# Narrow filler products in every softmax unit, and one tile's transposes and logits moved into the first dense layer

## The chip, the cores and the metric

The kernel runs on one core of a Trainium2 chip. The metric is the device time in microseconds of one execution; the time of a version is the median of its runs. Smaller is better. The engines are called PE (TensorE, matrix products), DVE (VectorE), ACT (ScalarE), POOL (GpSimd) and SP (SyncE, which here only issues DMAs).

## The reference

The input x has 8 sequences of 512 tokens with 1024 features, 4096 tokens in all, in f32. Four layers follow each other, each added to its input after a layer norm without weights:

```python
x = x + attn_a(layernorm(x), qkvw, qkvb, ow, ob)   # softmax attention, 32 heads of 32
x = x + ffn(layernorm(x), weight, bias, centroids, assignments)
x = x + attn_b(layernorm(x), bv_q, bv_k, bv_v)     # sigmoid attention, causal, 4 heads of 256
x = x + ffn(layernorm(x), weight, bias, centroids, assignments)
```

The two parts that the change touches are these:

```python
# attn_a
qkv = x @ attn_qkvw + attn_qkvb
scores = einsum('bhqd,bhkd->bhqk', q, k) / sqrt(32)
ctx = einsum('bhqk,bhkd->bhqd', softmax(scores), v)
out = ctx @ attn_ow + attn_ob
# ffn
dots = softmax(x @ centroids.T / 0.1)              # 64 clusters
hits = dots > 0.01
query_sel, cluster_sel = any(hits, axis=1), any(hits, axis=0)
row_sel = cluster_sel[assignments]
out = where(query_sel[:, None] & row_sel[None, :], x @ weight.T + bias, 0)
```

Which outputs of the first ffn layer are kept depends on the hits of all 4096 tokens. So no row of that layer can be finished before the last tile of 128 tokens has its logits, though its dense product can be begun.

## The kernel before, in words

**Stages.** The program is one body, `block_body`. It runs softmax attention with its output projection (to about 2673 us of the profiled execution), the first dense layer (about 2673 to 3000), the sigmoid attention, and the second dense layer. A tile is 128 tokens, there are 32 of them (0 to 31), four to a sequence.

**Products.** All big products (the q, k, v projections, the output projection, the dense layers) are in f32 and, after the first sequence, use a scheme with seven products for a two by two block product; `gather` adds their results up on DVE. In the code a "product" is one call of `nc.tensor.matmul` with 128 contracted rows. In the trace an f32 product is two passes, each a weight load and a matmul.

**The softmax loop** (L1003 on) goes over 64 units, one for four heads of one sequence. Unit n has four steps i. In step i, `rows_step` for unit n+1 (L873) makes the scores of 128 queries with all keys, and DVE takes their maxima (L874). `keys_step` for unit n (L901, L904) makes the scores of 128 keys with all queries, adds the maxima as a shift, and ACT takes exp of them (L906). Both use four matmuls side by side, on 32 rows of the array each, and share one PSUM buffer of four banks, `sc`, so each must wait until the other's scores are consumed. `values_step` (L928) and `normalize` (L940) make the context and the denominators; their matmuls are also four side by side, on 32 columns each. Once per unit, `turn_max` (L886 to L893) transposes the maxima, kept as three bf16 parts, through PE and copies them to SBUF.

**Filler.** Between those steps PE gets other work from a queue, `Filler`. Each piece has a weight, roughly its microseconds. The queue holds the projections of unit n+2 (`project_pieces`), the products of the output projection of the previous sequence (`out_products`), and for one finished tile at a time its norm, its transposes (L277) and its cluster logits, first by cluster (`logitsT`, L325), then by token (`logits`, L333). `filler.plan` splits a unit's queue over nine fillings by fixed shares, and the calls of `between` take them: in step 0 one before the turn of the maxima, one after it and one at the end of the step; in each other step one before `keys_step` and one after. The order of instructions on every engine is the program's order; nothing reorders it.

**Full and narrow form.** `product` (L548 to L556) writes a product either as one matmul on all 128 columns (L556) or, if the flag `narrow[0]` is set, as four matmuls on 32 columns each, side by side (L554). The flag is set by `between(False, form=...)` only for the fillings at the end of steps 0 and 2, which stand just after `values_step`, from unit 1 on. The transposes of `turn_max` and of tiles and the logits by token never go through `product`.

**The last output stage.** After the loop, four rounds (L1073 to L1089) do the output projection of the last two pairs of tiles (28 with 29, 30 with 31), with the pieces of the tiles that became ready. Round 0 has the tiles 26 and 27. Round 3 has 28 and 30. `filler.mix(pieces, first, step)` puts pieces into the queue at the given places. The tiles 29 and 31 are yielded at the end and laid among dense products by `to_rows` (L1403), whose list says which steps run and how many dense products follow them. A tile's transposes are copied by ACT into `nT`, which has one buffer; it leaves by a DMA from POOL's queue (L846), and only then can the next tile's copy start. The buffers of `ps_m` in PSUM, three of one bank, serve the products, the transposes and the logits alike. After the last logits, `rows_pieces` counts the hits, selects the rows, and the gates of the dense layer can begin.

Of the kernel before, what the change touches and what calls it, by code (L numbers as in the profile page):

```python
# [13 lines left out]
F32 = mybir.dt.float32  # L14
BF16 = mybir.dt.bfloat16
# [7 lines left out]
P = 128  # L23
# [3 lines left out]
TPB = S // P  # L27
NTILE = NT // P

HEADS_A, HD_A = 32, 32  # L30
# [6 lines left out]
NCL = 64  # L37
# [267 lines left out]
class Clusters:  # L305
# [5 lines left out]
        self.hits = fixed.tile([P, NCL], F32, name=f"hits_{name}")  # L311
        self.logits = {}

    def pieces(self, t, xT, later=None, width=NCL):

        nc, (b, i), st, ps_m = self.stage.nc, divmod(t, TPB), {}, self.stage.ps_m

        def by_cluster():  # L320
            acc = ps_m.tile([P, P], F32, tag="mm", name="logitsT")
            for c in range(NC):
                for j in range(NCL // width):
                    rows = ts(c % 2 * (NCL // width) + j, width)
                    nc.tensor.matmul(  # L325
                        acc[rows, :], self.cT[:, c, ts(j, width)], xT()[:, c, :], start=(c < 2), stop=(c >= NC - 2)
                    )
            st["lT"] = self.pool.tile([P, P], F32, tag="lT", name=f"lT_{self.name}_{t}")
            nc.scalar.copy(st["lT"], acc)

        def by_token():
            acc = ps_m.tile([P, NCL], F32, tag="mm", name="logits")
            nc.tensor.matmul(acc, st["lT"], self.stage.cst.twice, start=True, stop=True)  # L333
            if i == 0:
                self.logits[b] = self.pool.tile([P, TPB, NCL], F32, tag="lg", name=f"lg_{self.name}_{b}")
            nc.scalar.activation(self.logits[b][:, i, :], acc, AF.Copy, scale=INV_TEMP)
            if i == TPB - 1:
                steps = self.softmax(b)
                if later is None:
                    for step in steps:  # L340
                        step()
                else:
                    later(steps)

        return [(1.3, by_cluster), (0.25, by_token)]
# [61 lines left out]
def softmax_attention(tc, cst, stage, filler, clusters, pools, dr, late, args):  # L407
# [11 lines left out]
    nc, small, ps_m = tc.nc, stage.small, stage.ps_m  # L419
# [128 lines left out]
    narrow = [False]  # L548
# [281 lines left out]
    def tile_pieces(t, r, blocks=False):  # L830


        st = {}

        def xn():
            if "n" not in st:
                st["n"] = npool.tile([P, H], F32, tag="n1", name=f"n1_{t}")
            return st["n"]

        def xT():  # L840
            if "T" not in st:
                st["T"] = npool.tile([P, NC, P], F32, tag="nT", name=f"nT_{t}")
            return st["T"]

        def keep():
            nc.gpsimd.dma_start(dr.xT1[t], st["T"].rearrange("p c t -> p (c t)"))  # L846

        def box():
            if "box" not in st:
                st["box"] = npool.tile([P, NC, P], F32, tag="nT", name=f"nB_{t}")  # L850
            return st["box"]

        def fetch():
            nc.sync.dma_start(xT().rearrange("p c t -> p (c t)"), dr.xT1[t])

        if blocks:
            turn = stage.block_pieces(xn, box, dr.xT1[t]) + [(0.0, fetch)]
        else:
            turn = stage.turn_pieces(xn, xT, keep, vector=False)
        return (  # L860
            stage.norm_pieces(lambda: r, xn, scalar=True) + turn,
            clusters.pieces(t, xT, None if t >= NTILE - TPB else held.extend, width=HD_A),
        )

    def rows_step(n, qt):
# [10 lines left out]
    def split_max(n):  # L876

        st = state[n]
        part, rest = parts[n % 2], small.tile([P, TPB, GH], F32, tag="rest", name="rest")
        nc.vector.tensor_copy(part[:, :, :, 0], st["nmax"])  # L880
        nc.vector.tensor_tensor(rest, st["nmax"], part[:, :, :, 0], ALU.subtract)
        nc.vector.tensor_copy(part[:, :, :, 1], rest)
        nc.vector.tensor_tensor(rest, rest, part[:, :, :, 1], ALU.subtract)
        nc.vector.tensor_copy(part[:, :, :, 2], rest)

    def turn_max(n):  # L886

        st = state[n]
        tp = ps_m.tile([P, TPB, P], BF16, tag="mm", name="tpm")
        for qt in range(TPB):  # L890
            nc.tensor.transpose(tp[:, qt, :], parts[n % 2][:, qt, :, :].rearrange("p h c -> p (h c)"), cst.ident_h)
        st["shift"] = shiftp.tile([P, S], BF16, tag="shift", name=f"shift_{n}")
        nc.scalar.copy(st["shift"], tp.rearrange("p t q -> p (t q)"))  # L893

# [55 lines left out]

    places = [0]

    def between(sides=True, form=False):


        if sides:
            for _ in range(-(-len(side) // places[0])):
                side.popleft()()
            places[0] -= 1
        narrow[0] = form  # L960
        filler.take()
        narrow[0] = False

    def mix_tile(near, wait):
        norm, logits = tiles.popleft()(blocks=wait)
# [30 lines left out]
    pieces = project_pieces(1)  # L996
# [3 lines left out]
    run(enumerate(side))  # L1000
    side.clear()
    split_max(0)
    for n in range(units):  # L1003
        b, g = divmod(n, NC)
        ahead = n + 2
        if n == NC - 2:
            weights.fill(W_BUFS)
        if n == NC:
            ows.fill(OW_BUFS)
        count = 0  # L1010
        if n > NC:
            count = OUT_SHARES[(n - 1) % half] if n <= units - NC else LAST_SHARES[n - units]
        products = [next(outs) for _ in range(count)]
        if ahead < units:
            if g == NC - 2:
                side.extendleft(reversed(left_tasks(b + 1)))
            filler.add(weave(project_pieces(ahead), products), mark=ahead)
        else:
            filler.add(weave([], products))
        ready.extend(waiting)  # L1020
        waiting.clear()
        if tiles:
            mix_tile(n == units - 1, ahead < units)
        for c in OUT_SUMS.get(n, ()):
            side.extend(ow_sum_tasks(c))
        if b + 1 < B:
            if g == 0:
                norms = deque(norm_tasks(b + 1))
            if g < 2:
                run(enumerate(norms.popleft()))  # L1030
            if norms:
                side.extend(norms.popleft())
        side.extend(held)
        held.clear()
        filler.plan(FILLER_SHARES)
        places[0] = TPB + 1
        for i in range(TPB):
            if n + 1 < units:
                rows_step(n + 1, i)
            if i == 0 and n > 0:  # L1040
                sum_step(n - 1, TPB - 1)
            between()
            if i == 0:
                turn_max(n)
                between()
            if i == TPB - 1:
                sum_step(n, i - 1)
            keys_step(n, i)
            if i == 1:
                sum_step(n, i)  # L1050
            if i == 0 and n > 0:
                values_step(n - 1, 1)
                if ready:
                    by_cluster, by_token = ready.popleft()
                    run([by_cluster])
                    filler.mix([by_token], 6, 1)
                normalize(n - 1)
            if i == 2:
                values_step(n, 0)
            between(False, form=i in (0, 2) and n > 0)  # L1060
        if n + 1 < units:
            split_max(n + 1)
        if ahead < units:
            filler.until(ahead)
    sum_step(units - 1, TPB - 1)
    values_step(units - 1, 1)
    normalize(units - 1)
# [5 lines left out]
    for i, (start, end) in enumerate(((0, 4), (4, 8), (8, 10), (10, 14))):  # L1073
        ready = [make() for make in tiles]
        tiles.clear()
        for idx, k in order[start:end]:
            filler.add(last_pairs[k][0][idx])
            if idx == 0:
                filler.mix([last_pairs[k][2]], 2 + 4 * k, 1)
        for k, (norm, logits) in enumerate(ready):  # L1080
            filler.mix(norm[:2], 6 * k, 3)
            filler.mix(norm[2:], 11 + 8 * k, 2)
            filler.mix(logits, 15 + 8 * k, 3)
        filler.mix(late[i], 2, 4)
        filler.drain()
        run(enumerate(held))
        held.clear()
        if i < 3:
            yield  # L1089
    yield [make() for make in tiles]  # L1090


def ste_sign(nc, pool, w, n, name, hard):
# [234 lines left out]
def block_body(tc, long, dr, args, out):  # L1328
    x, xT_in, qkvw, qkvb, ow, ob, bv_q, bv_k, bv_v, wT, fbias, cT, assign = args
    nc = tc.nc  # L1330
# [66 lines left out]
    dense_stack = ExitStack()  # L1397
    dense1 = Dense(stage, weights, dense_pools(dense_stack), None, dr.xT1, dr.x1, hits1, sel)
    dense1.load_turned(0)
    (norm0, logits0), (norm1, logits1) = next(attention)  # L1400
    dense1.sums(0)
    dense1.load_turned(1)

    def to_rows(steps, hits, dense):
# [4 lines left out]
        for step, n in steps + [(count, 4), (rows, 3)]:  # L1409
# [4 lines left out]
    rest = [(0.0, step) for step in weight_sums[4:]]  # L1414
    left_over = to_rows(
        [
            (norm0[:2] + rest[:2], 8), (norm0[2:] + norm1[:1] + rest[2:], 4), (norm1[1:2] + logits0[:1], 3),
            (logits0[1:], 3), (norm1[2:], 3), (logits1[:1], 2), (logits1[1:], 8),
        ], hits1, dense1,
    )  # L1420
    a_outer.close()
# [228 lines left out]
```

## Time and profile before

| | us |
|---|---|
| median of 3 runs | 3823.99 (3821.19 to 3825.94) |
| the profiled execution, its own time | 3821.42 |
| its span, first to last instruction | 3819.7 |
| PE busy | 3760.0 (98%) |
| DVE busy | 2538.5 (66%) |
| ACT busy | 916.4 (24%) |
| POOL busy | 598.0 (16%) |

By stretch of the span, with what PE was busy in each:

| stretch, us | what runs | PE busy, us |
|---|---|---|
| 69 to 2598 | the softmax loop | 2506.96 of 2529 |
| 2598 to 2673 | the last output stage | 62.92 of 75 |
| 2673 to 3000 | the first dense layer | 325.73 of 327 |

The mean granted clock of PE was 0.998. PE executed 23,942 matmuls and as many weight loads. The start of a matmul in the trace is recorded and its end is modelled, so consecutive matmuls overlap in it; how fast they follow each other is read from their starts. In a timeline row, `128*32` means 128 active rows and 32 active columns of the array, and the size after it is that of the moving operand. A bracket at the end of a row gives idle time before it and what ended that.

### The profile page before, as it was taken

What the parts mean: (1) busy time and instruction counts of PE and PEld (TensorE: products, weight loads), DVE (VectorE), ACT (ScalarE), POOL (GpSimd) and SP (SyncE); (2) the same over time, 40 slices, a digit from 0 to 9 for tenths busy, and PEclk for the clock granted to TensorE, in tenths of its full rate; (3) what the DMA queues carried; (4) which work ended last, traced back from release to release, by engine and by line L of the source; (5) the groups of instructions that cost most, each with busy time, mean ns of one, the idle gap of its engine ahead of it and who ended that gap; (6) DMA issues with size and microseconds to landing.
All of it is one profiled execution on the core that took longest, in us unless ns stands there. A gap on an engine that the chain in (4) does not pass through costs nothing.

```text
span 3819.7 us, 58523 instructions
## 1 busy us (share of the span) xinstructions
PE 3760.0 (98%) x23942; PEld 2087.6 (55%) x23942; DVE 2538.5 (66%) x3495; ACT 916.4 (24%) x996; POOL 598.0 (16%) x585
## 2 busy tenths in 40 slices
PE   8999999999999999999999999998999999999999
PEld 4445555555555555555555555543444467774444
DVE  4767676767667667766866766665788844456556
ACT  1222222222222222222222222222111144430000
POOL 1222111111111111111111111111000045530000
PEclk9999999999999999999999999999999999999999
DMA  5335455645655455465455554356566665553332
GB/s 168 118 120 171 127 145 146 186 138 145 187 144 145 151 173 147 130 188 149 132 172 152 145 146 125 114 156 230 160 176 176 170 186 193 190 187 133 132 132 99
DMA packets 674490, 590.59 MB, mean 155 GB/s; under 512 B 268072, under 2 KB 519984, under 8 KB 674224
## 3 DMA queue, kind: packets, MB, share of 16 engines
q1 hardware_dynamic: 645120, 482.77, 44.4%
q0 software_dynamic: 24784, 88.36, 6.0%
q10 hardware_dynamic: 4320, 15.73, 1.0%
q8 instruction: 190, 3.11, 0.4%
q14 instruction: 76, 0.62, 0.1%
HBM read 452.48 MB, written 134.25 MB: 154 GB/s over the span
## 4 chain that ended last, share of the span: by engine, by line
PE 91%; DVE 6%; DMA 1%; issue 1%; ACT 0%; POOL 0%; SPq 0%; DVEq 0%; ACTq 0%; POOLq 0%
PE mm L556 34%; PE dense L1236 19%; PE sc L901 7%; PE sc L873 7%; PE mm L554 7%; PE av L928 6%; PE csc L1295 4%; PE o L1314 4%; PE logitsT L325 1%; PE sc L904 1%; DVE nmax L874 1%; PE den L940 1%; PE tp L277 1%; DVE sum L917 1%; DVE ln_st L227 1%
## 5 line engine op out<-in xcount | busy, mean ns | idle before, releaser
L874 DVE TENSOR_REDUCE nmax<-sc 128x4 f32<-128x2048 f32 x256 | 586.0, 2289 | 299.7 <-PE sc L873 299.7
L906 ACT ACTIVATE pT<-sc 128x2048 f32<-128x2048 f32 x256 | 480.8, 1878 | 1160.5 <-PE sc L904 1155.5
L915 POOL TENSOR_TENSOR sum<-pT,pT 128x1024 f32<-128x1024 f32 x128 | 304.9, 2405 | 765.2 <-ACT pT L906 723.4
L556 PE MATMUL mm<-xT,w 128*128 128x256 f32 x1716 | 416.4, 388 | 1.6 <-DVE rden L943 1.6
L556 PEld LDWEIGHTS mm<-xT,w 128*128 128x128 f32 x1716 | 312.8, 190 | 125.4 <-issue 35.3
L901 PE MATMUL sc<-qk,qk 32*128 32x512 f32 x2048 | 292.6, 641 | 15.1 <-DVE nmax L874 14.6
L917 DVE TENSOR_TENSOR sum<-sum,pT 128x2048 f32<-128x2048 f32 x128 | 292.0, 2282 | 0.8 <-ACT pT L906 0.8
L873 PE MATMUL sc<-qk,qk 32*128 32x512 f32 x2048 | 291.9, 640 | 0.2
L142 DVE TENSOR_TENSOR u<-dense,u 128x512 f32<-128x512 f32 x223 | 149.2, 686 | 185.4 <-PE dense L1236 168.4
L928 PE MATMUL av<-pT,v 128*32 128x512 f32 x2048 | 246.2, 598 | 0.0
L1236 PE MATMUL dense<-sum,s 128*128 128x512 f32 x512 | 232.1, 594 | 2.6 <-DVE s L1183 2.6
L556 PEld LDWEIGHTS mm<-w,xT 128*128 128x128 f32 x1640 | 192.6, 192 | 51.1 <-issue 41.2
L556 PE MATMUL mm<-s,w 128*128 128x256 f32 x852 | 204.6, 386 | 0.0
L556 PE MATMUL mm<-w,xT 128*128 128x128 f32 x1640 | 204.6, 278 | 0.0
L556 PEld LDWEIGHTS mm<-s,w 128*128 128x128 f32 x852 | 156.9, 190 | 68.2 <-issue 29.3
L144 DVE SCALAR_TENSOR_TENSOR qk<-mm,qkvb_s,qk 128x256 f32<-128x256 f32 x224 | 107.6, 480 | 124.9 <-PE mm L556 83.9
L556 PE MATMUL mm<-ow,ctxT 128*128 128x512 f32 x354 | 176.6, 616 | 0.3 <-DMA ow<-o_T 0.2
L1236 PE MATMUL dense<-wT_s,dT_b 128*128 128x512 f32 x384 | 171.4, 593 | 1.7 <-DMA dT_b<-xT 1.7
L1236 PE MATMUL dense<-wT_s,dT_a 128*128 128x512 f32 x384 | 171.0, 593 | 0.0
L556 PEld LDWEIGHTS mm<-w,s 128*128 128x128 f32 x1344 | 156.7, 192 | 19.4 <-issue 19.4
L556 PE MATMUL mm<-w,s 128*128 128x128 f32 x1344 | 166.8, 277 | 0.0
L1236 PEld LDWEIGHTS dense<-sum,s 128*128 128x128 f32 x512 | 96.4, 190 | 123.4 <-issue 112.3
(244 smaller groups left out, 4932.5 us busy)
## 6 DMA issues: line engine op xcount, KB each, us to landing
w<-in_qkvw SPq DMA_DIRECT2D x252, 256.0 KB, 3.0
ow<-o_T SPq DMA_DIRECT2D x240, 256.0 KB, 3.7
w<-qk_T SPq DMA_DIRECT2D x224, 256.0 KB, 2.7
ow<-in_ow SPq DMA_DIRECT2D x180, 256.0 KB, 3.2
w<-v_T SPq DMA_DIRECT2D x112, 256.0 KB, 2.7
x<-in_x SPq DMA_DIRECT2D x32, 512.0 KB, 4.9
dT_a<-xT SPq DMA_DIRECT2D x32, 512.0 KB, 5.9
x_a<-x SPq DMA_DIRECT2D x32, 512.0 KB, 6.8
```

Of the source, the lines that this page charges most:

```text
L554: nc.tensor.matmul(out[ts(j, HD_A)], lhsT[:, ts(j, HD_A)], rhs, **flags)
L556: nc.tensor.matmul(out, lhsT, rhs, **flags)
L873: nc.tensor.matmul(sc[:, h, :], st["q"][rows, ts(qt, P)], st["k"][rows, :], start=True, stop=True)
L874: nc.vector.tensor_reduce(st["nmax"][:, qt, :], sc, AX.X, ALU.max, negate=True)
L901: nc.tensor.matmul(sc[:, h, :], st["k"][rows, ts(kt, P)], st["q"][rows, :], start=True, stop=False)
L906: nc.scalar.activation(pT, sc, AF.Exp, scale=SCALE_A)
L915: nc.gpsimd.tensor_tensor(st["sum"][:, h, :], st["pT", 0][:, h, :], st["pT", 1][:, h, :], ALU.add)
L917: nc.vector.tensor_tensor(st["sum"], st["sum"], st["pT", kt], ALU.add)
L928: nc.tensor.matmul(st["av"][rows, :], st["v"][:, kt, rows], pT[:, h, :], start=(kt == 0), stop=(kt == TPB - 1))
L1236: nc.tensor.matmul(st["acc"], st["left"][LEFT[k]][:, c, :], self.w[RIGHT[k]][:, c, :], start=(c == 0), stop=(c == half - 1),)
L1295: nc.tensor.matmul(sc[:, AT_OFF[i] : AT_OFF[i] + n], k[:, c, ts(i, P)], xT[:, c, i * P :], start=(c == 0), stop=(c == 1),)
L1314: nc.tensor.matmul(acc[:, j - jj, :], at[:, start : start + P], self.v[b * TPB + i][:, cols], start=(i == 0), stop=(i == j),)
```

## The change

The flag `narrow[0]` is set before the loop and cleared after it, so all filler products of all units are in the narrow form; `between` loses its argument. `turn_max` uses `product` with the identity as the moving operand in place of PE's transpose, and its PSUM tile is f32 instead of bf16. The tiles of the softmax stage pass `product` on to `pieces`, which uses it for the logits by token. In the last output stage, the places where a tile's transposes and logits are put change, and tile 30's transposes and logits are held back from round 3 and yielded, to stand first in the list of `to_rows`. The counts of dense products in that list change with it: 35 places pass before the hits are counted, instead of 31.

```diff
-    def pieces(self, t, xT, later=None, width=NCL):
+    def pieces(self, t, xT, later=None, width=NCL, product=None):
...
-            nc.tensor.matmul(acc, st["lT"], self.stage.cst.twice, start=True, stop=True)
+            (product or nc.tensor.matmul)(acc, st["lT"], self.stage.cst.twice, start=True, stop=True)
...
-            clusters.pieces(t, xT, None if t >= NTILE - TPB else held.extend, width=HD_A),
+            clusters.pieces(t, xT, None if t >= NTILE - TPB else held.extend, HD_A, product),
...
-        tp = ps_m.tile([P, TPB, P], BF16, tag="mm", name="tpm")
+        tp = ps_m.tile([P, TPB, P], F32, tag="mm", name="tpm")
         for qt in range(TPB):
-            nc.tensor.transpose(tp[:, qt, :], parts[n % 2][:, qt, :, :].rearrange("p h c -> p (h c)"), cst.ident_h)
+            part = parts[n % 2][:, qt, :, :].rearrange("p h c -> p (h c)")
+            product(tp[:, qt, :], part, cst.ident_h, start=True, stop=True)
...
-    def between(sides=True, form=False):
+    def between(sides=True):
...
-        narrow[0] = form
         filler.take()
-        narrow[0] = False
...
     split_max(0)
+    narrow[0] = True
     for n in range(units):
...
-            between(False, form=i in (0, 2) and n > 0)
+            between(False)
...
             filler.until(ahead)
+    narrow[0] = False
     sum_step(units - 1, TPB - 1)
...
             filler.mix(norm[:2], 6 * k, 3)
-            filler.mix(norm[2:], 11 + 8 * k, 2)
-            filler.mix(logits, 15 + 8 * k, 3)
+            if (i, k) == (3, 1):
+                left_over = norm[2:], logits
+            else:
+                filler.mix(norm[2:], (13 if i < 3 else 9) + 8 * k, 2)
+                filler.mix(logits, (18 if i < 3 else 14) + 8 * k, 4)
...
-    yield [make() for make in tiles]
+    yield [left_over] + [make() for make in tiles]
...
-    (norm0, logits0), (norm1, logits1) = next(attention)
+    (turn, logits), (norm0, logits0), (norm1, logits1) = next(attention)
...
-            (norm0[:2] + rest[:2], 8), (norm0[2:] + norm1[:1] + rest[2:], 4), (norm1[1:2] + logits0[:1], 3),
-            (logits0[1:], 3), (norm1[2:], 3), (logits1[:1], 2), (logits1[1:], 8),
+            (norm0[:1] + turn + norm0[1:2], 5), (logits[:1] + rest[:2], 3), (logits[1:], 2), (norm0[2:] + norm1[:1] + rest[2:], 4), (norm1[1:2] + logits0[:1], 3),
+            (logits0[1:], 3), (norm1[2:], 4), (logits1[:1], 3), (logits1[1:], 8),
```

## The prediction

> **What bounds the kernel now.** I read the page's busy shares and chain first, then the waits of TensorE, then its timeline in one softmax unit and at the turn to the first dense layer.
>
> ```profile
> PE 3760.0 (98%) x23942; PEld 2087.6 (55%) x23942; DVE 2538.5 (66%) x3495; ACT 916.4 (24%) x996; POOL 598.0 (16%) x585
> PE 91%; DVE 6%; DMA 1%; issue 1%; ACT 0%; POOL 0%; SPq 0%; DVEq 0%; ACTq 0%; POOLq 0%
> q8 instruction: 190, 3.11, 0.4%
> PE sc L901 <- DVE nmax L874: 14.6, 12, 3.0
> ```
>
> PE is busy 98% and is 91% of the chain. Its longest wait is 14.6 us in 12 places. So the end is set by how closely PE's instructions follow each other, which the timeline shows (start, length, line, tiles, active rows*columns, size of the moving operand, count; a row's length overlaps the next, so I take differences of starts):
>
> ```profile
> 1517.33 1.92 PE L928 MATMUL av<-pT,v 128*32 128x512 f32 x16
> 1519.07 1.05 PE L554 MATMUL mm<-s,w 128*32 128x256 f32 x16
> 1519.93 1.06 PE L554 MATMUL mm<-w,xT 128*32 128x128 f32 x32
> 1520.92 1.14 PE L873 MATMUL sc<-qk,qk 32*128 32x512 f32 x8
> 1521.99 1.16 PE L556 MATMUL mm<-w,xT 128*128 128x128 f32 x8
> 1522.98 1.95 PE L556 MATMUL mm<-w,s 128*128 128x128 f32 x16
> 1524.77 1.06 PE L556 MATMUL mm<-w,xT 128*128 128x128 f32 x8
> 1525.76 1.14 PE L901 MATMUL sc<-qk,qk 32*128 32x512 f32 x8
> ...
> 1530.99 1.99 PE L556 MATMUL mm<-xT,w 128*128 128x256 f32 x8
> 1532.82 0.39 PE L891 MATMUL tpm<-ident_h,parts 128*128 128x128 bf16 x4
> 1533.04 1.95 PE L556 MATMUL mm<-xT,w 128*128 128x256 f32 x8
> 1534.92 1.14 PE L901 MATMUL sc<-qk,qk 32*128 32x512 f32 x8
> ```
>
> Three forms alternate: scores on 32 rows (R), full products (F), and products in four 32-column parts (C). An f32 product is two passes; a C pass is four instructions. The trace's starts, over all rows of the phase, give:
> - One pass of N=256 takes 216 ns and of N=512 429 ns in F and C alike. At N=128, F takes 112 (mean 111.7) and C 109.
> - R to either form costs 109 ns. Then F pays 104 ns on its first pass (1521.99 to 1522.98 is 0.99, 8x0.112 is 0.90); C pays 24 (1517.33 to 1519.07 is 1.74, 4x0.429 is 1.716).
> - Back to R: F pays 93 ns (1524.77 to 1525.76), C 113 (1519.93 to 1520.92 is 0.99, 8x0.109 is 0.872).
> - The turn of the maxima is 4x56 ns, and the F pass after it is 56 late: 1533.04 to 1534.92 is 1.88, 8x0.216 plus 0.093 plus 0.056.
>
> Then the turn to the dense layer:
>
> ```profile
> 2663.15 0.60 PE L277 MATMUL tp<-ident,n 128*128 128x128 f32 x4
> 2667.04 0.43 PE L333 MATMUL logits<-twice,lT_a 128*128 128x64 f32 x2 [3.29 <-ACT nT L279]
> 2667.53 1.93 PE L325 MATMUL logitsT<-nT,cT_s 128*32 128x128 f32 x32
> 2672.99 3.60 PE L1236 MATMUL dense<-wT_s,dT_a 128*128 128x512 f32 x8
> ```
>
> Tile 30's copies into nT wait for tile 28's nT to leave by DMA, and PE idles 3.29 us. The 32 matmuls after it take 1.93 us against 1.08 elsewhere: the windows show a clock of 0.74 there.
>
> [...] each change costs about 0.1 us, whichever two forms meet. [...] the first passes show 104 and 24. [...] the four of a C pass start 7 ns apart. [...] The full bf16 turn ran at 56 ns; no run here shows bf16 on 32 columns.
>
> **The change, part by part.** (a) *Narrow in all units.* Of a unit's nine fillings seven are F now, in six visits between R steps (the first two share one with the turn). Over 64 units the built order gives 378 R-to-F and 383 F-to-R changes, of which 3 each stay. The number of changes is the same afterwards[...]. Loads: 375x(104-24) = 30.0 us less. Way back: 380x(113-93) = 7.6 us more. Net -22.4.
>
> (b) *Pitch.* 3328 full N=128 passes become narrow: 3328x(111.7-109.2) = -8.3. The 2568 passes of N=256 and 700 of N=512 change by nothing; they are most of PE's time, and the C rows of before show the pitch is kept over 16 passes.
>
> (c) *Turn of the maxima.* Four bf16 transposes become four products of four parts, into f32. PE streams the same columns, and eight instructions 7 ns apart just fit in 56 ns: I take 4x56 and no delay after it[...], -64x56 = -3.6. Upper bound: the f32 pitch, 4x109, which is 64x(436-280) = +10.0 instead. The ScalarE copy stays 128x512 (0.59 us).
>
> (d) *Logits by token.* 25 of them stand in the loop: two passes of 56 ns, after which F waits 56 twice for its load. Narrow hides it: -2.8. Four tiles' transposes in the last units now stand between C rows: +0.2.
>
> Sum of PE in the loop: -22.4-8.3-3.6-2.8+0.2 = -36.9. Some is not kept: in about 26 places PE waits already (25 us in all), behind DVE or a copy that PE's gain does not hasten. A unit gains 0.58 us in 39; such a run of DVE work is some 10 us, so 26x0.15, about 4 us, goes into longer waits. Kept: -33. Of the L901 starts nine in ten stand 0.34 us or more after the reduce that frees their banks, more than one stretch gains.
>
> (e) *Last output stage.* Before, waits of 4.0 us lie at tiles 26 and 27 (1.84, 0.58, 0.99, 0.60). Moved two products later, their first transpose waits 0.4; the next still waits for DVE's L762 at 2606.2, and tile 27's copies for tile 26's DMA. I take -1.5. At the last part, tile 28's transposes go ahead by two products, but product 9 then needs the bank that DVE frees at 2657.26, wherever PE stands: eight products are done then, not ten. From there eight products (6.9), logits (1.4) and tile 30's transposes (0.9) reach the dense layer at 2666.5 instead of 2672.99: -6.5. Tile 30's logits, now inside it, return 1.5; the wait of 0.63 for tile 29 goes. Moved with tile 30 are two copies and one 512 KB DMA on POOL's queue; tile 29's root stands ahead of that DMA, so nothing on POOL is delayed. Sum -7.1.
>
> (f) *What is late next.* At the last logits 27 dense products are done, not 23. DVE's order does not move with them: softmax and hits, then the sums of pair 1, 6.6 us after the last logits (2697.97 to hits 2702.66, plus an addition and two sums). PE needs that sum after five products, 4.5 us: a new wait of 2.1. Then rows, gates and pair 2's sums: from the selection's copies to that sum 22.2 us before, 21.6 now; PE has 26 products from the count, not 30, and waits 1.9. Together +4.0, so this turn gives -3.1.
>
> Total -36. The profiled execution, 3821.4 us with a span of 3819.7, becomes 3785.4; the median of the three runs is 2.6 above it, so I forecast 3788.
>
> **The rivals.** *The turn is dear:* [...] 13.6 us less gain, 3802. [...] *The gain is taken up by waits:* DVE, 66% busy, sets the units, and the gain in the loop falls to about a third, 3809. Against: only 25 us of waits in 2,530, and L901's slack. *Slower, by instruction fetch:* the loop's PE instructions double, by the built order from 39,000 to 80,000, and q8 brings them in packets of 16 KB, 256 instructions of 64 bytes. A narrow N=128 pass takes 8 in 109 ns and empties a packet's worth in 3.5 us; 3728x8/256 = 116 such packets fall in N=128 work, where now one stretch is under 4 us. A packet took 0.9 to 1.8 us, 1.08 in the median. Were that exposed at each, +125: 3913. It decides from 36/116 = 0.31 us a packet. Against: narrow rows of 32 run at 109 with no gap, also where a fetch falls beside them. *It does not do what it says:* the built order shows the F rows of the loop turned into C, so this is out, save for a clock that falls under narrow work; ACT's and DVE's lengths and the clock (1.00) are the same in narrow stretches.
>
> **How the numbers follow.** Forecast, with its turn between 56 and 80 ns, 3788: 0.66. Dear turn, 3802: 0.14. Taken up, 3809: 0.12. Slower, 3913: 0.05. A clock or other loss that just cancels the gain, 3824: 0.03. Low end: the loop's gain kept whole (-36.9), no new waits in dense (-7.1), all 4.0 us at tiles 26 and 27 gone instead of 1.5, and the runs' own spread of 2.8: 3775. High end: the dear turn with 5 us of further waits, 3807. About 0.2% (7.6 us) is what a measurement can tell from no change: faster 0.92, same 0.03, slower 0.05.
>
> **What would show it.** Right: F rows of the loop gone to L554; first passes after R 24 ns late; N=128 at 109; turn and its successor 56 apart; nearly as many mode changes; the loop's last denominators about 33 us earlier; the 3.29 us gone, and two waits of dense for DVE's s of about 2 us. Wrong: gaps in PE that no semaphore ends, at block distances; a pitch of turn near 109; the wait of L901 for nmax grown by tens of us; a clock below 1.00 in the loop.

## The result, and the profile after

The changed kernel takes 3833.97 us (median of 17 runs, 3826.48 to 3839.74), the kernel before 3823.62 beside it (17 runs). The ratio is 1.0028, 95% interval 1.0022 to 1.0035: slower by about 10 us (0.3%), and 46 us above my forecast of 3788. The profiled execution took 3832.04, with a span of 3830.3 and a clock of 0.995 (before 3821.42, 3819.7, 0.998).

The lines of the page after, which answer to those of before:

```profile
PE 3742.1 (98%) x44666; PEld 1865.3 (49%) x44666; DVE 2539.7 (66%) x3495; ACT 916.3 (24%) x996; POOL 603.0 (16%) x585
q8 instruction: 352, 5.77, 0.6%
PE 88%; DVE 8%; issue 2%; DMA 1%; SPq 0%; ACT 0%; POOL 0%; DVEq 0%; ACTq 0%; POOLq 0%
```

PE is busy 17.9 us less, as it should be, and yet the end is later. In the chain "issue" is 2% where it was 1%: time in which PE waited for nothing that the profile shows. The instruction queue q8 brought 352 packets instead of 190. The waits of TensorE say where (us in total, times, longest):

```profile
PE mm L554 <- issue: 19.9, 14, 3.8
PE sc L902 <- DVE nmax L874: 16.9, 12, 2.9
PE dense L1239 <- DVE s L1186: 6.5, 4, 2.0
PE mm L556 <- DMA ow<-o_T: 4.1, 2, 3.4
PE sc L873 <- issue: 1.7, 1, 1.7
PE mm L556 <- DVE spare L762: 1.7, 1, 1.7
```

The wait for issue is new: before had none. First an undisturbed unit in TensorE's timeline, about the same place as the one shown of before:

```profile
1526.65 0.39 PE L905 MATMUL sc<-shift,ones_h 32*128 32x512 bf16 x4
1526.98 1.92 PE L929 MATMUL av<-pT,v 128*32 128x512 f32 x16
1528.72 1.05 PE L554 MATMUL mm<-s,w 128*32 128x256 f32 x16
1529.58 1.06 PE L554 MATMUL mm<-w,xT 128*32 128x128 f32 x32
1530.57 1.14 PE L873 MATMUL sc<-qk,qk 32*128 32x512 f32 x8
1531.64 1.08 PE L554 MATMUL mm<-w,xT 128*32 128x128 f32 x32
1532.54 1.93 PE L554 MATMUL mm<-w,s 128*32 128x128 f32 x64
1534.29 1.06 PE L554 MATMUL mm<-w,xT 128*32 128x128 f32 x32
1535.27 1.14 PE L902 MATMUL sc<-qk,qk 32*128 32x512 f32 x8
```

The three rows from 1531.64 to 1535.27 are 32 passes of N=128 and the way back: 3.63 us, where the full form took 3.77 (1521.99 to 1525.76). All prices came as forecast: the first C pass is 24 ns late, N=128 runs at 109, back to R costs 113.

Now the same kind of stretch beside the transfer of the rows (SP's timeline, then TensorE's):

```profile
469.69 0.38 SPq L526 DMA_DIRECT2D rows<-ln_rows  x1
```

```profile
470.21 1.96 PE L554 MATMUL mm<-w,xT 128*32 128x128 f32 x64
471.98 1.93 PE L554 MATMUL mm<-w,s 128*32 128x128 f32 x64
473.84 1.14 PE L902 MATMUL sc<-qk,qk 32*128 32x512 f32 x8
474.80 0.39 PE L905 MATMUL sc<-shift,ones_h 32*128 32x512 bf16 x4
475.12 1.28 PE L554 MATMUL mm<-w,xT 128*32 128x128 f32 x34
480.18 4.49 PE L554 MATMUL mm<-w,xT 128*32 128x128 f32 x94 [3.78 <-issue]
484.60 0.71 PE L873 MATMUL sc<-qk,qk 32*128 32x512 f32 x4
```

After 34 of 128 matmuls PE stands still for 3.78 us in the middle of a product, and no semaphore ends it. Then it runs slowly: 94 matmuls, 23.5 passes, take 4.42 us, against 2.56 at 109 ns. The page of the windows gives 0.89 as the clock from 470 to 486 (before 1.00), and 0.50 from 481 to 484. Shortly before the stop, `send` in `norm_tasks` (L526) writes 1,024 values of 4 bytes to DRAM, each a piece of its own. This is the traffic of 471 to 473:

```profile
DMA packets 1224, 0.34 MB, mean 172 GB/s; under 512 B 1065, under 2 KB 1065, under 8 KB 1223
...
q1 hardware_dynamic: 1223, 0.33, 75.8%
q8 instruction: 1, 0.02, 7.5%
```

1,065 of the 1,224 packets are small, and one brings instructions of PE: a fetch. In the trace's packet records it starts at 472.67 and takes 2.39 us; the median of all 352 is 1.01. Over the whole kernel the longest fetch took 4.19 us, beside another of these transfers; before 1.83. Yet a slow packet isn't the whole of the delay: this one is in at 475.06 and PE goes on at 480.18, and beside four of the seven transfers no fetch took longer than 1.83.

By stretch, from the starts in both traces, with what I had forecast:

| stretch | forecast | measured |
|---|---|---|
| softmax loop, first turn to last denominators | -33 | +8.0 (2527.9 to 2535.9) |
| from there to the first dense product | -8.0 | -6.15 (75.73 to 69.58) |
| the first dense layer | +4.9 | +6.7 |
| all after it | 0 | +1.8 |

In the loop most units gain 0.5 us each. Seven lose, those that send the rows (units 2, 10, 18, 26, 34, 42, 50, turn to turn): 4.6, 5.3, 3.9, 5.6, 2.8, 7.0 and 3.2, together +32.5 before rounding. Of the 15 waits for issue 14 lie at these places, 21.0 of 21.6 us.

### The profile page after: what moved, and what is told of

The parts are those of the page before. It is cut to its first block, busy times and chain, and to the rows that moved or that the text cites. A ratio compares the mean times of both kernels' runs of the same rounds, so it can differ in the third digit from the quotient of the medians.

```text
span 3830.3 us, 99991 instructions
## 1 busy us (share of the span) xinstructions
PE 3742.1 (98%) x44666; PEld 1865.3 (49%) x44666; DVE 2539.7 (66%) x3495; ACT 916.3 (24%) x996; POOL 603.0 (16%) x585
## 4 chain that ended last, share of the span: by engine, by line
PE 88%; DVE 8%; issue 2%; DMA 1%; SPq 0%; ACT 0%; POOL 0%; DVEq 0%; ACTq 0%; POOLq 0%
PE mm L554 37%; PE dense L1239 18%; PE sc L902 7%; PE sc L873 6%; PE av L929 6%; PE csc L1298 4%; PE o L1317 4%; PE mm L556 2%; DVE nmax L874 2%; PE logitsT L325 1%; PE sc L905 1%; PE den L941 1%; PE tp L277 1%; DVE sum L918 1%; DVE xT L534 0%
## 5 line engine op out<-in xcount | busy, mean ns | idle before, releaser
L554 PE MATMUL mm<-xT,w 128*32 128x256 f32 x7168 | 429.4, 382 | 1.8 <-DVE rden L944 1.7
L554 PE MATMUL mm<-s,w 128*32 128x256 f32 x5376 | 320.9, 380 | 4.3 <-DVE qk L144 3.8
L554 PEld LDWEIGHTS mm<-xT,w 128*32 128x32 f32 x7168 | 217.7, 110 | 220.1 <-issue 50.0
L902 PE MATMUL sc<-qk,qk 32*128 32x512 f32 x2048 | 292.1, 640 | 17.8 <-DVE nmax L874 16.9
L554 PEld LDWEIGHTS mm<-s,w 128*32 128x32 f32 x5376 | 167.4, 110 | 191.3 <-issue 64.9
L554 PE MATMUL mm<-w,xT 128*32 128x128 f32 x7168 | 228.5, 276 | 17.5 <-issue 17.0
L554 PEld LDWEIGHTS mm<-w,xT 128*32 128x32 f32 x7168 | 199.3, 111 | 80.9 <-issue 68.1
L554 PE MATMUL mm<-ow,ctxT 128*32 128x512 f32 x1792 | 213.3, 595 | 0.0
L144 DVE SCALAR_TENSOR_TENSOR qk<-mm,qkvb_s,qk 128x256 f32<-128x256 f32 x224 | 107.4, 480 | 123.5 <-PE mm L554 118.6
L554 PE MATMUL mm<-w,s 128*32 128x128 f32 x5376 | 162.9, 273 | 0.0
L554 PE MATMUL mm<-ow,c 128*32 128x512 f32 x1344 | 158.7, 594 | 0.0
```

Of the source, the lines that this page charges most:

```text
L554: nc.tensor.matmul(out[ts(j, HD_A)], lhsT[:, ts(j, HD_A)], rhs, **flags)
L902: nc.tensor.matmul(sc[:, h, :], st["k"][rows, ts(kt, P)], st["q"][rows, :], start=True, stop=False)
```

## The experiments

Theory A: PE's instructions come by DMA (the 352 packets of q8), and the narrow form at N=128 takes 8 in 109 ns. The 1,024 small pieces hold a fetch up; PE runs out of instructions, stands still, and its clock falls. Rival B: the DMA only happens to lie there, and the instruction stream stalls at such places anyway. Rival C: the loss is in the last stages, with the new waits for DVE.

**Move the transfer.** In `e1_send_later` the rows leave one step later, at the start of the next unit's list:

```diff
-            [root, shift, idle, idle, send],
-            [idle, idle, spread, idle, idle],
+            [root, shift, idle, idle, idle],
+            [send, idle, spread, idle, idle],
```

> The changed kernel with one edit: the small DMA that writes a sequence's norm rows (1024 elements of 4 bytes, once per sequence, 7 in all) leaves in the first step of unit 8b+3 instead of the last step of unit 8b+2, where PE runs its narrow N=128 passes. Theory A (a PE instruction packet is stuck behind those small DMA packets while narrow N=128 passes empty the store of instructions): the seven stalls without a semaphore go, about 4.8 us each with the slow clock after them, so about 34 us less, near 3800, and the clock of the loop is back at 1.00. Rival B (narrow N=128 passes alone outrun the fetch, or the clock is lowered by narrow work): the stalls stay, 3834 within 4. Rival C (the loss lies in the dense layer): also 3834.

It took 3811.31 (5 runs), ratio 0.9968 [0.9955, 0.9980]: 22.7 us less than the changed kernel, by moving seven DMAs of 4 KB. On the line of the filler the wait for issue falls to a sixth:

```profile
PE mm L554 <- issue: 3.3, 5, 1.6
```

The loop is 17 us shorter than before. It isn't the whole 34 us: five of the seven units 8b+3, which now hold the transfer, lose 1.1 to 2.4 us where their like gain 0.5. The transfer now lies beside passes of N=256 too, which use instructions half as fast (8 in 216 ns); that fits what is left, but this edit alone can't show it.

**Send more.** `e2_send_more` sends the rows twice again, to a tensor that nobody reads, at the ends of units 8b+4 and 8b+6.

```diff
...
-            scaled[:4],
+            scaled[:4] + [again],
             scaled[4:],
+            [idle] * 4 + [again],
...
```

> The changed kernel with the same rows sent again, to a spare buffer, in the last step of the units 8b+4 and 8b+6, which also run narrow N=128 passes: 14 more DMAs of 1024 elements of 4 bytes. Theory A: most of these 14 places get a stall like the seven, 3 to 5 us each, so 40 to 65 us more, near 3885. Rival B: no more than the DMAs' own issue, 3834 to 3838.

It took 3913.05 (4 runs), ratio 1.0243 [1.0226, 1.0260], 79 us more, where I expected 40 to 65. TensorE's waits (line numbers are 4 higher):

```profile
PE mm L558 <- issue: 49.3, 52, 2.7
...
PE mm L558 <- DVE qk L144: 9.0, 9, 1.2
...
PE sc L877 <- issue: 7.1, 3, 3.1
```

This speaks against B: the stalls come where the DMA comes. But the edit also lengthens the list of small tasks in those units, and a second line has grown, the wait for DVE's L144 (3.8 in the changed kernel). So the same edit was made in the kernel before.

**The same DMAs under the full form.** `e6_before_more` is the kernel before with that edit.

> The kernel before, with the rows sent a second and third time in units 8b+4 and 8b+6 (14 more DMAs of 1,024 pieces of 4 bytes), as e2_send_more does with the changed kernel, where it cost 79 us. If the loss needs PE's doubled instructions, nothing: 3824 to 3828. If such a DMA holds up PE's stream or another engine in any form, 3824 + 14 x 5.6 = 3902.

3837.04 (5 runs), ratio 1.0039 [1.0026, 1.0052]: 13.6 us, more than I expected, but a sixth of the 79.

```profile
PE mm L560 <- issue: 1.4, 1, 1.4
PE mm L558 <- DVE qk L144: 8.9, 11, 1.1
```

One wait for issue in the whole run, 1.4 us. The wait for DVE's L144 was this in the kernel before:

```profile
PE mm L554 <- DVE qk L144: 2.8, 6, 0.5
```

It grew to 8.9, as in e2, so this cost comes with the edit's shifted tasks in either form; the rest of the 13.6 I didn't trace. Three fetches in this run took 3.1 to 3.7 us beside the added DMAs, and PE didn't stop at them: in the full form a late fetch can stay hidden. What is left of e2 for its 14 DMAs is 79.1 - 13.6 = 65.5, which is 4.7 us each. The seven of the changed kernel cost 5.2 each, as worked out below.

**Few large pieces.** In `e5_rows_large` DVE turns the eight columns of values, so that they leave in 32 pieces of 128 bytes, at the same place:

```diff
-            st["rows"] = small.tile([P, 2, TPB], F32, tag="ln_rows", name="ln_rows")
+            both = xpool.tile([P, H], F32, tag="x", name=f"wide_{b}")
+            st["wide"], st["turned"] = both[:, :32], both[:, 32:64]
+            nc.vector.memset(st["wide"], 0.0)
+            st["rows"] = st["wide"][:, : 2 * TPB].rearrange("p (k t) -> p k t", k=2)
...
-            nc.sync.dma_start(dr.rows[b].rearrange("(k t p) -> p k t", k=2, p=P), st["rows"])
+            nc.vector.transpose(st["turned"], st["wide"])
+            to = dr.rows[b].rearrange("(r j c) -> j r c", j=4, c=32)
+            for j in range(4):
+                nc.sync.dma_start(to[j], st["turned"][32 * j : 32 * j + 2 * TPB, :])
```

> The changed kernel, but the 1,024 values of the layer norm (rows) are turned by DVE in blocks of 32 by 32 and leave in 32 pieces of 128 bytes instead of 1,024 pieces of 4 bytes, at the same place. If the small packets hold up PE's instruction fetch, the seven stalls of about 5.6 us in units 8b+2 go whole: 3834 - 39 = 3795 (3791 to 3800), with the softmax loop about 31 us shorter than in the changed kernel's 2536. If the place in the instruction stream makes the stall, and the DMA only happens to lie there, 3834; if any DMA of 4 KB at that place does it, 3811 to 3834.

3796.74 (5 runs), ratio 0.9933 [0.9921, 0.9945]: 37 us below the changed kernel. B falls. All 352 fetches are still there (0.6% of the DMA engines' time), none takes over 2.06 us, and the wait for issue is all but gone. TensorE's waits, then its timeline at the place of the stall (line numbers are 6 higher):

```profile
PE mm L560 <- issue: 0.7, 3, 0.3
```

```profile
472.90 0.39 PE L911 MATMUL sc<-shift,ones_h 32*128 32x512 bf16 x4
473.23 3.70 PE L560 MATMUL mm<-w,xT 128*32 128x128 f32 x128
476.86 1.14 PE L879 MATMUL sc<-qk,qk 32*128 32x512 f32 x8
```

The 128 matmuls that took 9.48 us in the changed kernel (475.12 to 484.60) take 3.63.

**Slow the instructions instead.** `e7_full_there` leaves the rows in small pieces, but keeps the N=128 filler, and with it the turn of the maxima, in the full form in the seven units that send them.

```diff
-        if narrow[0]:
+        if narrow[0] and not (narrow[0] == 2 and rhs.shape[-1] == P):
...
+        narrow[0] = 2 if g == 2 and b + 1 < B else 1
```

> The changed kernel with the rows sent as they are, but in the seven units that send them the filler products of N=128 stay in the full form; all others are narrow. If the stall needs the rate of instructions of narrow N=128 passes, it goes there: 3834 - 39 = 3795, plus 2 to 4 for the narrow form's gain lost in these units: 3797 to 3801. If the DMA alone, or the narrow products of N=256 and 512, make it, 3834.

3800.57 (5 runs), ratio 0.9941 [0.9929, 0.9954], and 0.4 us of waiting for issue. The stretch after the same DMA in TensorE's timeline:

```profile
473.81 0.39 PE L905 MATMUL sc<-shift,ones_h 32*128 32x512 bf16 x4
474.13 3.84 PE L556 MATMUL mm<-w,xT 128*128 128x128 f32 x32
477.90 1.14 PE L873 MATMUL sc<-qk,qk 32*128 32x512 f32 x8
```

32 matmuls instead of 128 for the same work, and no stop. So the loss needs both: the small pieces, and the narrow form at N=128 beside them. Taking away either one gives back 33 to 37 us.

The places of the stops point to instructions as what PE lacks, at least in part of them. Its matmuls, weight loads and semaphore instructions come to 256 for each packet of q8: 90,195 for 352 packets in the changed kernel, 48,728 for 190 before. I counted them in order and divided the number of the instruction with which PE goes on after a stop by 256. The remainder is 191 to 194 in 5 of the 15 stops of the changed kernel, in 8 of the 13 in `e9_pool_queue` (below), and in all four that are left in e5 and e7; by chance it would be so in 1 of 64. These stops lie whole packets apart, as they would if PE had used up one packet and had to wait for the next. What holds PE in the other stops, inside a packet, this doesn't show.

**Is the cure a gain by itself?** `e10_before_large` puts the large pieces into the kernel before.

> The kernel before with the rows in 32 pieces of 128 bytes, as in e5_rows_large. If that edit only takes away a stall which the narrow form brought in, the kernel before gains nothing: 3821 to 3825. If the small packets cost the kernel before as well, some of the 37 us that e5 gained over the changed kernel show here: 3800 to 3815.

3822.15 (13 runs) against 3824.06, ratio 0.9996 [0.9988, 1.0005]: nothing. So the 37 us are lost, and won back, only with the narrow form.

**Another queue.** `e9_pool_queue` sends the small pieces from POOL's queue (`nc.gpsimd.dma_start` for `nc.sync.dma_start` in `send`).

> The changed kernel with the rows' 1,024 pieces of 4 bytes sent at the same place from POOL's queue instead of SP's. If the small packets hold the fetch up in the 16 DMA engines[...], the stalls stay: about 3834 (3825 to 3840). If it is SP's ring that holds the fetch back, they go: 3797, as with the large pieces.

3822.92 (12 runs), ratio 0.9997 [0.9988, 1.0005]: between the two, so neither expectation. Most of the stalls stay:

```profile
PE mm L554 <- issue: 14.9, 13, 4.2
```

That speaks against SP's own queue as the only place. That the small pieces and the fetches meet in the DMA engines is my estimate: the packet records name queues (q1 for the pieces, q8 for the fetches in the changed kernel) and no engine, so no run shows it. Why the loss is 11 us smaller here isn't settled. The pieces also start at other moments from POOL's queue, and by how much the stalls depend on that wasn't tried.

**The two parts alone.** `e3_loop_only` has the narrow loop and the old end; `e4_tail_only` has the old loop and the new end.

```diff
# e3_loop_only, against the changed kernel
-    yield [left_over] + [make() for make in tiles]
+    yield [make() for make in tiles]
...
-            (norm0[:1] + turn + norm0[1:2], 5), (logits[:1] + rest[:2], 3), (logits[1:], 2), (norm0[2:] + norm1[:1] + rest[2:], 4), (norm1[1:2] + logits0[:1], 3),
+            (norm0[:2] + rest[:2], 8), (norm0[2:] + norm1[:1] + rest[2:], 4), (norm1[1:2] + logits0[:1], 3),
```

(and the places in the last rounds with it; e4 is the reverse, made in the kernel before).

> The kernel before with the loop's part of the change alone: narrow form in all units, the turn of the maxima and the logits by token as products; the last output stage and the dense layer as before. By the two traces the loop is 8 us longer and the rest about 2 us longer, so theories A and B expect about 3832; rival C (the dense layer has the loss) expects 3795.

> The kernel before with the other part alone: tile 30's transposes and logits moved into the first dense layer and the places of the other tiles' pieces changed. By the two traces: the stretch from the loop's last denominators to the first dense product is 6.2 us shorter, the dense layer 6.7 longer, so 3824 within 3. My prediction for this part was 3.1 less, 3821. Rival C: about 3860.

The loop alone: 3830.72 (17 runs), ratio 1.0018 [1.0011, 1.0026]. The tail alone: 3825.62 (13 runs), ratio 1.0004 [0.9995, 1.0012]. C falls: the loop makes the loss. The tail is no gain, where I had forecast 3 us; how, the trace of dense shows below.

**The best version.** `e8_rows_large_old_tail` is e5 with the end of the kernel before.

> e5_rows_large with the last output stage and the turn to the dense layer as in the kernel before. The tail part alone measured 3825.6 against 3823.7, so it loses 2: 3793 if e5 gives 3795. If the tail part gains once the loop is faster, as I forecast with 3.1 us, it is 3 us above e5 instead.

3795.63 (5 runs, 3790.55 to 3796.50), ratio 0.9924 [0.9912, 0.9936]: some 28 us faster than the kernel before and 38 faster than the changed one. From e5 it can't be told apart (1.1 us, the intervals overlap), so with the faster loop too the new tail brings nothing that shows.

## Why the prediction was wrong

The step that failed is the judgement on my rival "slower, by instruction fetch": in the sum of the forecast the fetch stands at nothing, and in the runs its stalls cost 36.7 us. I had the mechanism, gave it 0.05, and dismissed it with "narrow rows of 32 run at 109 with no gap, also where a fetch falls beside them". That is true and stayed true: in e5 all 352 fetches together leave 0.7 us of waiting. But it holds for a fetch that takes the usual 1 us. I took the 0.9 to 1.8 us of before as what a fetch costs, and didn't ask what other DMA traffic runs beside it. The price in the rival (1.08 us at each of 116 packets) was wrong as well: the cost is nothing at almost all of them and some 5 us at seven.

The page and the trace of before had the warning. First the rows' own time to landing, then the line of a weight load on the page:

```profile
DMA to landing us min/median/max: 10.0/10.6/11.7
```

```profile
w<-qk_T SPq DMA_DIRECT2D x224, 256.0 KB, 2.7
```

4 KB took 10.6 us where 256 KB took 2.7. In the changed kernel PE goes on at 480.18, 10.5 us after the issue at 469.69. At all seven places the stops that begin within 10 us of the issue are over 8.9 to 10.5 us after it, about when such a transfer lands (10.0 to 11.7 us before, 9.0 to 10.9 in e7). Which step between the fetched packet and PE the transfer holds back, the records don't show. Under the full form the 32 passes that follow take 64 instructions (weight loads and matmuls), under the narrow one 256 in the same time, a whole packet.

Point by point, in the order of the prediction:

- **(a), (b) narrow form and pitch.** The prices are right. The first C pass is 24 ns late (F 104 before), way back 113, pitch 109; that the 24 and 104 are the time of a weight load was my reading, the traces show the delays alone. An undisturbed unit gains 0.5 us against 36.9/64 = 0.58 forecast. What was left out is the stall: the seven units lose 32.5 in all, and in e8 the same units gain 4.2, so it costs 36.7, or 5.2 each. The waits for issue show 21.0 of it. Most of the rest is the slow running after them, as at 480.18: at five of the seven places the trace has the clock at one half for 3.4 us.
- **(c) the turn.** bf16 on 32 columns runs at 56 ns, and the next pass isn't late. The dear turn is out; its 4x109 was my estimate from the f32 pitch, since no trace of before has bf16 on 32 columns.
- **Gain kept.** In e8, without the stalls, the loop is 28.0 us shorter, in e5 25.9; forecast 33. The growth of the waits that I took as 4 us is there: in e8 PE's wait for nmax is 16.9, before 14.6, that for DVE's L144 3.7, before 2.8. Besides, units 1 and 6 are 1.5 us longer instead of 0.5 shorter; in e10, in the full form, they are 1.8 and 1.7 longer too, so that needn't be the narrow form's doing. What it comes from, I didn't follow up.
- **(e) the last output stage.** -6.15 where I said -8.0. The waits at tiles 26 and 27 fell from 4.0 to 2.4, as forecast, but this 1.5 doesn't reach the end: PE's waits for the DMA of `ow` grew from 3.0 to 4.1, and the bank that L762 frees comes 60.3 us after the last denominators, before 60.1. My sum was wrong there, since its 6.5 already took the time of that bank as fixed. From the bank to the dense layer are 9.3 us, where I had 9.2. The 3.29 us wait is gone, as forecast. In its stead product 9 of the last part waits for the bank that L762 frees, also as forecast:

```profile
2662.66 1.02 PE L556 MATMUL mm<-ow,ctxT 128*128 128x512 f32 x2
2663.52 0.60 PE L277 MATMUL tp<-ident,n 128*128 128x128 f32 x4
2665.78 1.98 PE L556 MATMUL mm<-ow,ctxT 128*128 128x512 f32 x4 [1.66 <-DVE spare L762]
...
2675.05 3.60 PE L1239 MATMUL dense<-wT_s,dT_a 128*128 128x512 f32 x8
```

One pair of traces doesn't give this stretch to a microsecond: it took 72.9 to 75.7 us in five traces with the old end and 67.1 to 71.4 in seven with the new one.

- **(f) the new waits.** 1.98 and 1.92 us, where I had 2.1 and 1.9. What I left out is what follows a wait:

```profile
2734.08 3.60 PE L1239 MATMUL dense<-wT_s,dT_a 128*128 128x512 f32 x8
2739.59 5.40 PE L1239 MATMUL dense<-sum,s 128*128 128x512 f32 x8 [1.92 <-DVE s L1186]
2744.83 1.45 PE L1239 MATMUL dense<-wT_s,dT_a 128*128 128x512 f32 x3
```

The eight passes ahead of the last row took 5.24 us (2739.59 to 2744.83), where eight take 3.43 (429 ns each): in the trace's starts four of them stand 802 to 854 ns apart, and the clock records have 0.50 for 3.41 us from 2740.60. At the start of the second dense layer the same happens after a wait of 1.88 us, another 1.7. These two make +6.7 out of +4.9, and nearly all of the +1.8 at the end.

Together: of the 46.7 us between forecast and trace, 36.7 are the seven stalls, 4.3 the smaller gain in the rest of the loop, 1.9 the last output stage, and 3.6 the slow passes after waits in dense; 0.2 lie ahead of the loop.

## What to carry to other kernels

PE's instructions came by DMA here (queue q8: 352 packets of 16 KB for 90,195 instructions, 256 each): when a change multiplies an engine's instructions, look for the densest stretch, count how long one fetched packet lasts there (256 instructions at 8 in 109 ns are 3.5 us), and see what other DMA traffic runs then. A small transfer with a long time to landing (4 KB in 10.6 us) was the one to suspect here, and harmless until the change; send it in large pieces (37 us back here) or away from the dense stretch (23 us back, one step later). Price a new wait on PE above its length: at two places here about 1.7 us more were lost to half speed after a wait of 1.9.

## What was not expected of the hardware

- After waits of 1.8 to 2.1 us at the dense layers PE's next passes sometimes ran at half speed (853 ns for 429), mostly for 3.4 us, and sometimes not, at the same place in different runs: after 1.91 us four or more slow ones in the tail-only kernel, none in e5. The traces' clock records have such a stretch at 0.50 for 3.41 us (twice that in one case, in e5); the two in the changed kernel's dense layers begin at 2740.60 and 3423.27. At the first wait of the second dense layer it came in one of the five traces with the old tail and in six of the seven with the new one. Why isn't settled.
- A DMA of 1,024 pieces of 4 bytes can delay another queue's packets: fetches up to 4.19 us in the changed kernel and 9.88 in e2, against 2.06 at most in e5 with the 32 pieces. In the twelve traces every fetch over 2.7 us starts within 11 us of such a DMA's issue.
